# A four-layer graph network on one core: seven products for the first weight, and sums by adding DMA transfers for the third

## The chip, the core and the metric

The kernel runs on one core of a Trainium2 chip. The metric is device time in microseconds. One launch computes everything, from the inputs in the chip's memory to the output. TensorE (PE in the profile) multiplies matrices, with its weight loads shown as PEld; VectorE (DVE), ScalarE (ACT) and GpSimd (POOL) work elementwise; SyncE (SP) and GpSimd issue transfers (DMA). Each engine takes its own instructions in order, and waits for the others by semaphores.

## The reference

The input x is 128 graphs of 64 nodes with 256 features, fp32, and one 64 x 64 matrix `adj` is shared by all graphs. Four layers follow one another, each as `x = layernorm(x + layer(x))`. The change touches layer 0, and the computation of eigenvectors that is threaded into it and used in layer 1:

```python
def _slconv(x, adj, S, W):
    support = jnp.einsum('bnf,fh->bnh', x, W)
    weighting = adj * S                        # S is adj itself here
    return jnp.einsum('nm,bmh->bnh', weighting, support)

def layer0(x):
    h = relu(_slconv(x, adj, adj, W1))         # 256 -> 512
    h = relu(_slconv(h, adj, adj, W2))         # 512 -> 1024
    return _slconv(h, adj, adj, W3)            # 1024 -> 256

def layer1(x):
    deg = sum(A, 0) + sum(A, 1) - diagonal(A)
    L_norm = d_inv_sqrt[:, None] * (diag(deg) - A) * d_inv_sqrt[None, :]
    _, U = eigh(L_norm)                        # 64 x 64
    agg = einsum('mn,bnd->bmd', U.T, x)
    return einsum('nm,bmd->bnd', U, relu(agg @ W1 + b1) @ W2 + b2)
```

Layer 2 is a chain of graph convolutions and short LSTMs, layer 3 an attention among the nodes of a graph. Their instructions on PE, DVE and ACT stand in the same order before and after the change.

## The kernel before

**Groups.** Layer 0 works through 16 groups of 512 rows of x (8 graphs), in the order 4 to 15, then 0 to 3. A group goes through: `burst` (mixing by `adj`² over the nodes, which also transposes; 64 small matmuls in bursts) into `m1`; the first weight, `weigh`, into `h1` with a relu; `burst` into `m2`; the second weight into `h2`, with a relu; the third weight into `s3`; `mix_rows` (mixing again), the residual sum, and the layernorm in pieces (`scalar_norm`, seven pieces: five on ACT, one on POOL). The group g + 1 is interleaved with group g: its `burst` into `m1` stands in the middle of the second weight of g, its first weight among the products of the third weight of g, its `burst` into `m2` after that.

**Seven products.** The second weight (in two halves, `j` = 0 and 1) and the third are multiplied as 2 x 2 blocks by seven products in place of eight, with sums of blocks formed ahead by DVE: `sums_second` for the second weight, and for the third four sums of 1024 elements a partition out of `h2` (`sh[:, 0]`, `sh[:, 1]`, `H21` and `H12` in `layer0`). The sums of the weights are formed once (`sums_of_weights`). `seven` issues the products in the order 1, 2, 6, 5, 7, 3, 4. Products 1, 6, 7 and 4 add up in one PSUM bank (`ch`), 5 and 3 in another (`b5`), 2 has one of the four `ps` banks. Between them the partial results are taken out: ACT copies product 1 to block c11; DVE adds product 2 to it, and ACT applies the relu; ACT copies `ch` after product 6 to c12; ACT copies product 5 to c22; DVE adds `ch` after product 7 to c22; DVE adds product 3's to c12; and ACT takes `ch` after product 4 to c21. The first weight is not done so: per group it is eight matmuls of 512 columns. The last two groups' third weight (`PLAIN` = 2) is done by plain products, `plain`.

**Order.** In layer 0, the order of instructions on PE, DVE and ACT is the order in which the program gives them. `step` puts the eviction of a product behind the matmuls of the next one, and then appends one piece of the norm. Instructions of POOL and SP go to their own queues in the order in which they are given.

**Eigenvectors.** `eigen` computes U on the same engines: 62 steps of a tridiagonalisation (about 24 small DVE operations and one matmul pair each), six passes of bisection, recurrences, and a tail that ends with `u2` and `ut2`, which layer 1's first matmuls read. It is a Python generator. `mm` (L965) adds the stated time of each matmul to a clock `now`; `between` (L955) then lets `eigen` go on when the time that it last asked for has been reached. That time is what the DVE operations given so far sum up to by *stated* times: `Timed` (L42) adds `least` (0.25 us, 0.285 in the bisection, 0.22 in the recurrence) for each, plus a term for long ones. So stated times decide between which matmuls the operations stand, not how long they take.

In the profile L52 is any DVE operation of `eigen` or of layer 0, L966 any matmul given by `mm`, L1031 the matmuls of `burst`, L312 and L323 the matmuls of `eigen`, L162 any instruction of layers 1 to 3, L975 a relu, L1070, L1077 and L1081 the copies of `seven`, L1037 the copies of `burst`. Names in groups leave out buffer numbers: `m` is m1 or m2, `h` is h1 or h2, `aw` the weights, `tw` and `tv` sums of weights, `ss` and `sh` sums of blocks.

## Time and profile before

| | us |
|---|---|
| median of three timed runs (lowest to highest) | 2280.58 (2280.14 to 2281.84) |
| the profiled execution, its own time | 2277.23 |
| its span (first to last instruction) | 2275.4 |
| granted TensorE clock, mean | 0.995 |
| layer 0's matmuls in the span | about 25 to 828 |
| one group of layer 0 (from 309.90 to 360.37, the same products of two groups) | 50.47 |

The page cuts the span into 40 slices and gives each engine's busy share in tenths. Slices 1 to 14 are layer 0:

```profile
PE   8999999999999989999999999999999999999997
PEld 6888888887788778999999999999999999999985
DVE  5888777776888879765967977977877887578977
ACT  3444444443434435665655655655656555566554
POOL 0000000000000010000100000000010010000012
PEclk9999999999999999999999999999999999999999
DMA  7000000000000031000111211211221211001331
```

Two rows of its costliest groups show how layer 0's products are listed. The columns are line, engine, operation, output and inputs, shapes and count; then busy us in total and mean ns of one; then the idle time just before them with what ended most of it:

```profile
L966 PE MATMUL ch<-m,tw 128*128 128x256 f32 x512 | 124.7, 381 | 3.1 <-ACT h L1077 1.7
L966 PE MATMUL b<-ss,aw 128*128 128x256 f32 x512 | 121.9, 379 | 0.0
```

A matmul of fp32 leaves two records, so x512 are 256 matmuls.

### The profile page before, as it was taken

The numbers are of one execution on the slowest core, as the hardware profiler recorded it, in microseconds if no ns is written. First come the engines' busy times: TensorE is split into PE (matmuls) and PEld (weight loads), VectorE is DVE, ScalarE is ACT, GpSimd is POOL, SyncE is SP. The second block draws the span as 40 slices with busy tenths as digits, with TensorE's granted clock in tenths as the row PEclk, the third lists the DMA queues.
The fourth block names the chain that finished last, engine by engine and source line by source line (L and its number), as shares of the span: only waits on it lengthen the run. The fifth ranks groups of instructions, "written<-read, shape, count | busy, mean of one in ns | idle before, by whom it ended". The sixth has DMA issues, their size and how long they took to land.

```text
span 2275.4 us, 52244 instructions
## 1 busy us (share of the span) xinstructions
PE 2233.0 (98%) x20612; PEld 1990.8 (87%) x20612; DVE 1772.5 (78%) x5868; ACT 1189.5 (52%) x2892; POOL 137.0 (6%) x315
## 2 busy tenths in 40 slices
PE   8999999999999989999999999999999999999997
PEld 6888888887788778999999999999999999999985
DVE  5888777776888879765967977977877887578977
ACT  3444444443434435665655655655656555566554
POOL 0000000000000010000100000000010010000012
PEclk9999999999999999999999999999999999999999
DMA  7000000000000031000111211211221211001331
GB/s 245 11 11 11 11 11 11 11 20 11 11 11 1 1 126 57 11 11 20 66 40 48 78 57 50 87 57 41 87 66 40 78 66 39 31 21 65 117 107 59
DMA packets 80117, 107.93 MB, mean 47 GB/s; under 512 B 23296, under 2 KB 64256, under 8 KB 79872
## 3 DMA queue, kind: packets, MB, share of 16 engines
q1 hardware_dynamic: 79520, 104.32, 14.1%
q8 instruction: 162, 2.65, 0.5%
q14 instruction: 83, 0.68, 0.1%
q10 hardware_dynamic: 352, 0.28, 0.0%
HBM read 57.64 MB, written 45.09 MB: 45 GB/s over the span
## 4 chain that ended last, share of the span: by engine, by line
PE 91%; DVE 6%; issue 1%; ACT 1%; DMA 1%; POOL 0%; SPq 0%; ACTq 0%; DVEq 0%; POOLq 0%
PE ps L162 58%; PE ch L966 14%; PE ps L966 10%; PE b L966 7%; PE ps L1031 2%; PE pa L312 1%; DVE w L162 1%; DVE D L52 1%; DVE tw L52 1%; DVE X L162 1%; DVE gates L162 0%; DVE st L162 0%; DVE v L162 0%; ACT gates L162 0%; DVE h L52 0%
## 5 line engine op out<-in xcount | busy, mean ns | idle before, releaser
L162 PE MATMUL ps<-w,wih 128*128 128x128 f32 (+2 forms) x2944 | 572.0, 298 | 0.3 <-ACT gates L162 0.3
L162 PE MATMUL ps<-w,sums 128*128 128x128 f32 (+2 forms) x3104 | 476.3, 293 | 0.1
L162 PEld LDWEIGHTS ps<-w,wih 128*128 128x128 f32 x2944 | 453.1, 191 | 26.5 <-issue 6.8
L162 PEld LDWEIGHTS ps<-w,sums 128*128 128x128 f32 x3104 | 422.7, 191 | 14.3 <-ACT gates L162 1.9
L162 ACT ACTIVATE gates<-gates,cbi 128x256 f32<-128x256 f32 (+4 forms) x736 | 314.0, 479 | 171.8 <-DVE gates L162 169.9
L162 DVE TENSOR_TENSOR gates<-gates,ps 128x512 f32<-128x512 f32 (+4 forms) x408 | 233.7, 583 | 171.1 <-PE ps L162 158.0
L162 ACT COPY gates<-ps 128x512 f32<-128x512 f32 (+4 forms) x408 | 204.2, 506 | 252.3 <-PE ps L162 245.4
L162 PE MATMUL ps<-hs,whh 128*128 128x128 f32 (+1 forms) x896 | 181.2, 284 | 0.1
L162 PE MATMUL ps<-w,whh 128*128 128x128 f32 (+1 forms) x896 | 181.2, 284 | 0.0
L162 ACT ACTIVATE gates<-ps,cbi 128x128 f32<-128x128 f32 (+2 forms) x368 | 119.5, 384 | 42.9 <-PE ps L162 42.5
L162 PEld LDWEIGHTS ps<-hs,whh 128*128 128x128 f32 x896 | 139.8, 191 | 0.3 <-DVE hs L162 0.3
L162 PEld LDWEIGHTS ps<-w,whh 128*128 128x128 f32 x896 | 139.8, 191 | 0.0
L975 ACT ACTIVATE h<-h 128x512 f32<-128x512 f32 x96 | 60.5, 630 | 150.9 <-DVE h L52 150.9
L966 PE MATMUL ch<-m,tw 128*128 128x256 f32 x512 | 124.7, 381 | 3.1 <-ACT h L1077 1.7
L966 PE MATMUL b<-ss,aw 128*128 128x256 f32 x512 | 121.9, 379 | 0.0
L966 PE MATMUL ps<-aw,m 128*128 128x512 f32 x256 | 116.0, 606 | 1.5 <-DMA aw<-in_a_w_dram 1.5
L966 PEld LDWEIGHTS ch<-m,tw 128*128 128x128 f32 x512 | 94.9, 190 | 18.6 <-DVE h L52 3.4
L966 PEld LDWEIGHTS b<-ss,aw 128*128 128x128 f32 x512 | 96.8, 190 | 12.9
L162 POOL TENSOR_SCALAR rs<-mv 128x2 f32<-128x2 f32 x96 | 23.5, 255 | 1325.1 <-DVE mv L162 1323.7
L966 PEld LDWEIGHTS ps<-aw,m 128*128 128x128 f32 x256 | 48.3, 194 | 55.7 <-issue 51.4
L1037 ACT COPY m<-ps 128x512 f32<-128x512 f32 x96 | 51.2, 587 | 75.5 <-PE ps L1031 75.0
L162 PE MATMUL ps<-hs,sums 128*128 128x128 f32 (+1 forms) x448 | 90.6, 284 | 0.0
(373 smaller groups left out, 4139.2 us busy)
## 6 DMA issues: line engine op xcount, KB each, us to landing
far<-w SPq DMA_DIRECT2D x42, 512.0 KB, 2.9
w<-far SPq DMA_DIRECT2D x168, 128.0 KB, 3.1
X<-rest SPq DMA_DIRECT2D x24, 512.0 KB, 3.3
out_dram<-X SPq DMA_DIRECT2D x64, 128.0 KB, 1.8
rest<-XA SPq DMA_DIRECT2D x12, 512.0 KB, 2.6
rest<-X SPq DMA_DIRECT2D x12, 512.0 KB, 2.8
XA<-in_x_dram SPq DMA_DIRECT2D x22, 256.0 KB, 6.9
aw<-in_a_w_dram SPq DMA_DIRECT2D x3, 1024.0 KB, 10.2
```

The costliest lines, as they stand in the source:

```text
L52: return getattr(self.engine, name)(out, *args, **kw)
L162: getattr(e, name)(*[real(x) for x in args], **{k: real(v) for k, v in kw.items()})
L312: PE.matmul(out, lhsT, rhs, start=True, stop=True)
L966: PE.matmul(out, lhsT, rhs, start=start, stop=stop, **kw)
L975: S.activation(dst, src, AF.Relu)
L1031: PE.matmul(p[h][m, k, t, :], src[hs, t, f], sqT2[hs, hs], start=True, stop=True)
L1037: S.copy(to[:, h, c:c + 2], p[h])
```

## The change

- **First weight.** For the first weight of every group but the first in order, `seven` with `by_first` takes the place of `weigh`: products of 2 matmuls of 256 columns, 14 in all in place of 8 of 512. The blocks are quarters of `m1` (X11 to X22) and of W1. DVE forms sums of the blocks in `sums_first` (three operations of 256 elements) and one more (into X12) after product 2. Product 5 gets a `ps` bank. The seven products stand between products 2 and 5 of the third weight of the group before.
- **Third weight.** DVE's four sums are gone. ACT writes -H11 and -H12 (`less`, four operations a group) into two slots of `sh`; SP copies two blocks into the other slots (512 KB each); and five transfers of 512 KB a group, issued by GpSimd, add blocks in place (`adds`). `h2` is laid out again so that a block is contiguous in a partition. The order of its products becomes 1, 2, 5, 6, 7, 3, 4, and the two `burst`s into `m2` stand one place apart from before: after products 6 and 4. One group, not two, is done by `plain`.
- **Sums of weights.** Those of the second weight move ahead by two steps of the first weight, and those of the first weight are added after the first half of the second weight of the first group. The third's signs differ (`signed_sums`).
- **Eigenvectors.** The stated times go from 0.25 to 0.21, from 0.285 to 0.278, from 0.22 to 0.21 (layer 0's own operations stay at 0.25). In the tail, operations stand in another order, two squares become one operation, and the two last matrices are spread one at a time.

```diff
@@ -44,7 +44,7 @@
-        self.engine, self.free, self.until, self.least = engine, free, until, 0.25
+        self.engine, self.free, self.until, self.least = engine, free, until, 0.21
...
@@ -557,7 +557,7 @@
-    V.least = 0.285
+    V.least = 0.278
...
@@ -599,14 +599,14 @@
-    V.least = 0.22
+    V.least = 0.21
     for k in range(1, N):
-    V.least = 0.25
+    V.least = 0.21
...
@@ -704,29 +704,32 @@
+    V.tensor_copy(t1, pl)
+    pp_ = (yield from rows(co_[7], 1, "pa"))[:, 0, :]
+    there, until[0] = until[0], 0.0
     V.reciprocal(t0, t0)
     V.tensor_mul(t0, t0, C["off"])
-    V.tensor_copy(t1, pl)
     V.tensor_mul(t1, t1, t1)
     V.tensor_reduce(co_[8], t1, AX.X, ALU.max)
...
+    until[0] = max(until[0], there)
+    yield soon()
     rowdot(hs, pp_, t0)
     V.tensor_scalar(hs, hs, -1.0, 1.0, op0=ALU.mult, op1=ALU.add)
-    V.tensor_mul(hs, hs, hs)
-    V.tensor_mul(hs, hs, co_[8])
-    yield soon()
-    V.tensor_scalar(co_[9], s1, s1, 2.0, op0=ALU.mult, op1=ALU.mult)
...
     V.tensor_scalar(UT, pu, co_[12], None, op0=ALU.mult)
+    V.memset(u2, 0.0)
+    V.memset(ut2, 0.0)
     yield full()
+
+    def spread(out, lhsT):
+        p2 = ps([2 * N, N], "pa")
+        for h in range(2):
+            mm(p2[h * N:(h + 1) * N, :], lhsT, C["eye"])
+        for h in range(2):
+            V.tensor_copy(out[h * N:(h + 1) * N, h * N:(h + 1) * N], p2[h * N:(h + 1) * N, :])
+
+    spread(u2, UT)
     pt = ps([N, N], "pa")
     PE.transpose(pt, UT, C["eye"])
     until[0] = now[0] + 0.7
     U = cp.tile([N, N], F32, name="U")
     V.tensor_copy(U, pt)
-    V.memset(u2, 0.0)
-    V.memset(ut2, 0.0)
     yield full()
-    for out, lhsT in ((u2, UT), (ut2, U)):
-        p2 = ps([2 * N, N], "pa")
-        for h in range(2):
-            mm(p2[h * N:(h + 1) * N, :], lhsT, C["eye"])
-        for h in range(2):
-            V.tensor_copy(out[h * N:(h + 1) * N, h * N:(h + 1) * N], p2[h * N:(h + 1) * N, :])
+    spread(ut2, U)
 
 
 ROWS = 8192
...
-PLAIN = 2
@@ -983,24 +989,31 @@
     B11, B12, B21, B22 = (aw2[:, r:r + 2, c:c + 512] for r in (0, 2) for c in (0, 512))
     tw = wa.tile([P, 3, 2, 512], F32, name="tw")
     D11, D12, D21, D22 = (aw3[:, r:r + 4, c:c + P] for r in (0, 4) for c in (0, P))
-    tv = wa.tile([P, 4, 4, P], F32, name="tv")
+    tv = wa.tile([P, 5, 4, P], F32, name="tv")
+    W11, W12, W21, W22 = (aw1[:, r, c:c + 256] for r in (0, 1) for c in (0, 256))
+    tu = wa.tile([P, 3, 256], F32, name="tu")
     m1 = pa.tile([P, 2, 512], F32, name="m1")
     h1 = pa.tile([P, 4, 512], F32, name="h1")
     m2 = pa.tile([P, 4, 512], F32, name="m2")
     ss = pa.tile([P, 3, 2, 256], F32, name="ss")
-    h2 = pa.tile([P, 8, 512], F32, name="h2")
-    sh = pa.tile([P, 2, 4, 256], F32, name="sh")
+    h2 = pa.tile([P, 2, 8, 256], F32, name="h2")
+    sh = pa.tile([P, 4, 4, 256], F32, name="sh")
+    sx = pa.tile([P, 2, 256], F32, name="sx")
     s3 = pa.tile([P, 4, D], F32, name="s3")
     A11, A12, A21, A22 = (m2[:, k:k + 2, r:r + 256] for r in (0, 256) for k in (0, 2))
-    H11, H12, H21, H22 = (h2[:, c:c + 4, r:r + 256] for r in (0, 256) for c in (0, 4))
+    H11, H12, H21, H22 = (h2[:, r, c:c + 4, :] for r in (0, 1) for c in (0, 4))
 
 
     second = ((None, B11, B21, B22, tw[:, 2], B12, tw[:, 1], tw[:, 0]),
               (None, A11, A12, ss[:, 2], A22, ss[:, 0], ss[:, 1], A21))
-    third = ((None, D11, D21, D22, tv[:, 2], tv[:, 3], tv[:, 1], tv[:, 0]),
-             (None, H11, H12, H12, H22, sh[:, 0], sh[:, 1], H21))
+    third = ((None, D11, D21, tv[:, 4], tv[:, 2], tv[:, 3], tv[:, 1], tv[:, 0]),
+             (None, H11, H12, sh[:, 3], H22, sh[:, 0], sh[:, 1], sh[:, 2]))
+    X11, X12, X21, X22 = (m1[:, k, r:r + 256] for r in (0, 256) for k in (0, 1))
+    first = ((None, W11, W21, W22, tu[:, 2], W12, tu[:, 1], tu[:, 0]),
+             (None, X11, X12, X12, X22, sx[:, 0], sx[:, 1], X21))
     free = [0.0]
     VL = Timed(V, free, now)
+    VL.least = 0.25
     spare = [lambda: tl(pa, [P, D], "spare")]
     pending = []
 
@@ -1021,6 +1034,25 @@
         VL.tensor_sub(w[5], b12, w[1])
         VL.tensor_sub(w[6], w[3], w[5])
         VL.tensor_sub(w[4], w[2], w[6])
+
+    def signed_sums():
+        w = third[0]
+        VL.tensor_sub(w[7], D12, D22)
+        VL.tensor_sub(w[5], D12, D11)
+        VL.tensor_sub(w[6], D22, w[5])
+        VL.tensor_sub(w[4], D21, w[6])
+        VL.tensor_scalar(w[3], D22, -1.0, None, op0=ALU.mult)
+
+    def sums_first():
+        VL.tensor_add(sx[:, 0], X21, X22)
+        VL.tensor_sub(sx[:, 1], sx[:, 0], X11)
+        VL.tensor_sub(X21, X11, X21)
+
+    def less(slot, j, c):
+        S.activation(sh[:, slot, 2 * j:2 * j + 2], h2[:, 0, 4 * c + 2 * j:4 * c + 2 * j + 2, :], AF.Identity, scale=-1.0)
+
+    def adds(out, src):
+        nc.gpsimd.dma_start(out, src, accum_op=ALU.add)
 
     def burst(dst, src, c):
         to = dst.rearrange("p c (t h n) -> p h c t n", h=2, n=N)
@@ -1051,11 +1083,15 @@
 
         return product
 
+    def by_first(out, i, new):
+        w, a = (x[i] for x in first)
+        chained(out, [[(a[:, r * P:(r + 1) * P], w)] for r in range(2)], new)
+
     def by_third(out, i, new):
         w, a = (x[i] for x in third)
         chained(out, [[(a[:, k, r * P:(r + 1) * P], w[:, k, :]) for k in range(4)] for r in range(2)], new)
 
-    def seven(n, product, c11, c12, c21, c22, last):
+    def seven(n, product, c11, c12, c21, c22, last, order=(1, 2, 6, 5, 7, 3, 4), five="b5"):
 
         def view(b):
             return b[:, :2 * n].rearrange("p (i n) -> p i n", i=2)
@@ -1066,35 +1102,22 @@
                 relu(dst, dst)
 
         ch = view(bank("ch"))
-        product(ch, 1, True)
-        step(lambda: S.copy(c11, ch))
-        yield
-        b2 = view(bank())
-        product(b2, 2, True)
-        step(lambda: add(c11, b2))
-        yield
-        product(ch, 6, False)
-        step(lambda: S.copy(c12, ch))
-        yield
-        b5 = view(bank("b5"))
-        product(b5, 5, True)
-        step(lambda: S.copy(c22, b5))
-        yield
-        product(ch, 7, False)
-        step(lambda: add(c22, ch))
-        yield
-        product(b5, 3, False)
-        step(lambda: add(c12, b5))
-        yield
-        product(ch, 4, False)
-        step(lambda: last(c21, ch))
-        yield
+        for i in order:
+            if i in (2, 5):
+                b = view(bank("ps" if i == 2 else five))
+                b2, b5 = (b, None) if i == 2 else (b2, b)
+            out = {2: b2 if i == 2 else None, 5: b5 if i == 5 else None, 3: b5 if i == 3 else None}.get(i, ch)
+            product(out, i, i in (1, 2, 5))
+            step({1: lambda: S.copy(c11, ch), 2: lambda: add(c11, b2), 6: lambda: S.copy(c12, ch),
+                  5: lambda: S.copy(c22, b5), 7: lambda: add(c22, ch), 3: lambda: add(c12, b5),
+                  4: lambda: last(c21, ch)}[i])
+            yield i
 
     def plain():
         for t in (0, 2):
             p = bank().rearrange("p (t f) -> p t f", t=2)
             for i in range(2):
-                run(p[:, i, :], [(h2[:, c, (t + i) * P:(t + i + 1) * P], aw3[:, c, :]) for c in range(8)])
+                run(p[:, i, :], [(h2[:, t // 2, c, i * P:(i + 1) * P], aw3[:, c, :]) for c in range(8)])
                 step((lambda p=p, t=t: S.copy(s3[:, t:t + 2, :], p)) if i else None)
                 yield
         for _ in range(3):
@@ -1131,40 +1154,55 @@
         step()
         for t in range(4):
             weigh(t)
+            if t == 1:
+                sums_of_weights(second[0], B12)
         step()
-        sums_of_weights(second[0], B12)
         for c in (0, 2):
             burst(m2, h1, c)
         step()
         for g in range(n):
             sums_second()
             for j in range(2):
-                q = [h2[:, 4 * c + 2 * j:4 * c + 2 * j + 2, r:r + 256] for r in (0, 256) for c in (0, 1)]
-                for _ in seven(256, by_second(j), *q, relu):
-                    pass
+                q = [h2[:, r, 4 * c + 2 * j:4 * c + 2 * j + 2, :] for r in (0, 1) for c in (0, 1)]
+                for i in seven(256, by_second(j), *q, relu):
+                    if g == n - 1:
+                        continue
+                    if i == 5:
+                        less(2, j, 0)
+                    if i == 4:
+                        less(3, j, 1)
+                    if j and i == 7:
+                        nc.sync.dma_start(sh[:, 1], sh[:, 2])
+                    if j and i == 3:
+                        nc.sync.dma_start(sh[:, 0], H22)
+                        adds(sh[:, 1], H22)
+                    if j and i == 2:
+                        sums_first()
                 if j == 0 and g + 1 < n:
                     burst(m1, rows_of(order[g + 1]), 0)
                 if j == g == 0:
-                    sums_of_weights(third[0], D12)
-            q = [s3[:, r:r + 2, c:c + P] for r in (0, 2) for c in (0, P)]
-            w3 = seven(P, by_third, *q, S.copy) if g < n - PLAIN else plain()
-            next(w3)
-            next(w3)
-            if g < n - PLAIN:
-                VL.tensor_add(sh[:, 0], H21, H22)
-                VL.tensor_sub(sh[:, 1], sh[:, 0], H11)
-            for t in range(4):
-                if g + 1 < n:
-                    weigh(t)
-                if t == 0 and g < n - PLAIN:
-                    VL.tensor_sub(H21, H11, H21)
-                    VL.tensor_sub(H12, H12, sh[:, 1])
-            for _ in range(4):
+                    sums_of_weights(first[0], W12)
+                    signed_sums()
+            if g == n - 1:
+                for _ in plain():
+                    pass
+            else:
+                q = [s3[:, r:r + 2, c:c + P] for r in (0, 2) for c in (0, P)]
+                w3 = seven(P, by_third, *q, S.copy, order=(1, 2, 5, 6, 7, 3, 4))
                 next(w3)
-            if g + 1 < n:
+                for slot in range(3):
+                    adds(sh[:, slot], H21)
+                adds(sh[:, 3], sh[:, 1])
+                next(w3)
+                q = [h1[:, r:r + 2, c:c + 256] for r in (0, 2) for c in (0, 256)]
+                for i in seven(256, by_first, *q, relu, five="ps"):
+                    if i == 2:
+                        VL.tensor_sub(X12, X12, sx[:, 1])
+                next(w3)
+                next(w3)
                 burst(m2, h1, 0)
-            next(w3)
-            if g + 1 < n:
+                for _ in range(3):
+                    next(w3)
                 burst(m2, h1, 2)
             for t in (0, 2):
                 mix_rows(g, t)
-    nc = bacc.Bacc("TRN2", target_bir_lowering=False, num_devices=1, dynamic_dma_scratch_size=1024)
+    nc = bacc.Bacc("TRN2", target_bir_lowering=False, num_devices=1, dynamic_dma_scratch_size=1536)
```

More of the change, by code (lines that the diff above doesn't have):

```diff
@@ L712, in eigen @@
     V.tensor_scalar(co_[8], co_[8], nrm, (8.0 * 2.0 ** -24) ** 2, op0=ALU.mult, op1=ALU.mult)
-    pp_ = (yield from rows(co_[7], 1, "pa"))[:, 0, :]
+    yield soon()
+    V.tensor_scalar(co_[9], s1, s1, 2.0, op0=ALU.mult, op1=ALU.mult)
+    V.tensor_scalar(co_[10], s2e, s2e, 2.0, op0=ALU.mult, op1=ALU.mult)
+    V.tensor_tensor(co_[10], co_[10], co_[8], ALU.is_gt)
+    V.tensor_scalar(co_[11], s2e, 0.0, -2.0, op0=ALU.is_gt, op1=ALU.mult)
+    V.tensor_scalar(co_[11], co_[11], co_[10], 1.0, op0=ALU.mult, op1=ALU.add)
+    yield soon()
+    V.tensor_scalar(co_[12], s1, 0.0, -2.0, op0=ALU.is_gt, op1=ALU.mult)
+    V.tensor_scalar(co_[12], co_[12], 1.0, co_[11], op0=ALU.add, op1=ALU.subtract)
+    V.tensor_mul(co_[12], co_[12], rn)
+    V.tensor_mul(co_[11], co_[11], rn)
+    until[0] = max(until[0], there)
+    yield soon()
     rowdot(hs, pp_, t0)
     V.tensor_scalar(hs, hs, -1.0, 1.0, op0=ALU.mult, op1=ALU.add)
-    V.tensor_mul(hs, hs, hs)
-    V.tensor_mul(hs, hs, co_[8])
-    yield soon()
-    V.tensor_scalar(co_[9], s1, s1, 2.0, op0=ALU.mult, op1=ALU.mult)
+    V.tensor_scalar(hs, hs, hs, co_[8], op0=ALU.mult, op1=ALU.mult)
     V.tensor_tensor(co_[9], co_[9], hs, ALU.is_gt)
-    V.tensor_scalar(co_[10], s2e, s2e, 2.0, op0=ALU.mult, op1=ALU.mult)
-    V.tensor_tensor(co_[10], co_[10], co_[8], ALU.is_gt)
-    yield soon()
-    V.tensor_scalar(co_[11], s2e, 0.0, -2.0, op0=ALU.is_gt, op1=ALU.mult)
-    V.tensor_scalar(co_[11], co_[11], co_[10], 1.0, op0=ALU.mult, op1=ALU.add)
-    V.tensor_scalar(co_[12], s1, 0.0, -2.0, op0=ALU.is_gt, op1=ALU.mult)
-    V.tensor_scalar(co_[12], co_[12], 1.0, co_[11], op0=ALU.add, op1=ALU.subtract)
     V.tensor_scalar(co_[12], co_[12], co_[9], co_[11], op0=ALU.mult, op1=ALU.add)
-    V.tensor_mul(co_[12], co_[12], rn)
     yield full()
```

## The prediction

> **What bounds the kernel now.** I read the page's totals, then the windows of layer 0 (the only part whose instructions change: the order of the planned part, L162, is the same in both programs on PE, DVE and ACT), then the chain of waits, and last the timeline of one group and of layer 0's two ends.
>
> ```profile
> PE 2233.0 (98%) x20612; PEld 1990.8 (87%) x20612; DVE 1772.5 (78%) x5868; ACT 1189.5 (52%) x2892; POOL 137.0 (6%) x315
> PE 91%; DVE 6%; issue 1%; ACT 1%; DMA 1%; POOL 0%; SPq 0%; ACTq 0%; DVEq 0%; POOLq 0%
> ...
> core 0: us, PE busy (x) PEld busy (x) DVE busy (x) ACT busy (x) POOL busy (x), PEclk, DMA share, GB/s
> 57.00:541.00 484.00, 484.00 (x4319) 402.13 (x4319) 384.64 (x1794) 214.46 (x570) 20.33 (x56) 1.00 0.03 11
> 541.00:826.00 285.00, 282.35 (x2291) 230.65 (x2289) 237.89 (x874) 116.28 (x265) 14.21 (x37) 1.00 0.04 13
> 826.00:835.00 9.00, 4.59 (x48) 2.76 (x51) 7.17 (x35) 2.69 (x9) 1.08 (x3) 0.94 0.88 323
> ```
>
> From 57 to 541 TensorE has no gap at all, at a granted clock of 1.00; DVE is at 79% and ACT at 44%. Columns removed from TensorE are therefore time gained, one for one, as long as nothing takes a wait's place. At 826 to 835 TensorE is half idle: the eigenvectors come last. Prices of matmuls, from the chain of waits (start, us, what; the count is of records, two per matmul):
>
> ```profile
> 309.90 8.65 PE ps L966 x32
> 320.56 1.79 PE b L966 x16
> 334.17 1.73 PE ps L966 x8
> 812.36 13.81 PE ps L966 x64
> ```
>
> 1.73 is four matmuls of 256 columns (a product of the second weight). 1.79 is eight of 128 (one of the third). 8.65 is the third's product 2 and the four steps of the first weight together, so the first weight is 8.65 - 1.79 = 6.86 a group. 13.81 is a third weight without the seven products.
>
> **What the Trainium skill says.** "DMA: Bandwidth & Descriptors", section "Anatomy of one DMA — SWDGE (gpsimd) path", fits 2.0 us plus bytes/436e3 per transfer: 3.2 us for 512 KB. The trace agrees roughly, though on another queue: its 512 KB copies from SP take a median 2.9 us. The same page, "SWDGE vs HWDGE vs iDMA", says that adding transfers come from GpSimd only; that is how the change issues them. "Collectives: The Full Stack", "The bandwidth ceiling: the fold count and why AG ≠ RS ≠ AR", puts a reduction at half the rate of a copy, since each sum reads two sources. No run here shows it; it gives my estimate of an add's pace below. "SBUF — State Buffer", section "SBUF: two separate sides", warns that DVE can hold up the writing of GpSimd's descriptors. No trace here shows that either; it belongs to the second rival.
>
> **The change part by part.** Sums are against the profiled execution, 2277.23 us (span 2275.4); the median shown is 2280.58, so 3.35 is added at the end.
>
> First weight by seven, 15 groups (the first keeps the old way): a product is two matmuls of 256 columns, half of 1.73, and seven are 6.05. Gain 15 x (6.86 - 6.05) = 12.2. Group 14's third weight by seven: 13.81 - 7 x 1.79 = 1.3. TensorE loses 13.5 us of work.
>
> Its new waits. A product lasts 0.865 us now, half of the second weight's, but its evictions are as long as before. How the same order behaves there:
>
> ```profile
> 384.49 1.89 PE L966 MATMUL ps<-m,aw 128*128 128x256 f32 x8
> 387.06 0.67 DVE L52 TENSOR_TENSOR h<-h,ps 128x512 f32<-128x512 f32 x1
> 387.77 0.63 ACT L975 ACTIVATE h<-h 128x512 f32<-128x512 f32 x1 [2.00 <-DVE h L52]
> 388.31 0.49 ACT L810 ACTIVATE spare<-XA,sn_nm 128x256 f32<-128x256 f32 x1
> 388.93 0.57 ACT L1077 COPY h<-ch 128x512 f32<-128x512 f32 x1
> 391.39 1.89 PE L966 MATMUL b<-ss,aw 128*128 128x256 f32 x8
> ```
>
> Product 2 ends at 386.2. DVE's add follows at 387.06, ACT's relu 0.71 later, and what stands behind the relu on ACT 0.54 later still; ACT works in order. Behind it stands the copy of product 6 out of bank ch (0.57), and product 7 writes that bank. In the second weight product 7 begins 6.9 us in and never waits. In the first weight it is due at 3.47 (four products), while the copy ends at s + 0.71 + 0.54 + 0.6 and some 0.05 for the signal, s + 1.9, where s is the start of DVE's add, counted from the first product. DVE is late there: before the add stands the new subtraction into X12, which must wait until product 2 has read X12 (1.73, and 0.27 as DVE follows TensorE elsewhere: 2.00), then 0.30 for itself, then in 13 of the 15 groups two to five operations of the eigenvectors, 0.38 to 1.14 by their own rows. So s = 2.3 + (0 to 1.14), and TensorE stands for s - 1.55: 1.1 to 1.9 us with the eigenvectors beside it, 0.74 without. Over the 15 groups, by the operations that stand in the new program at each, 19.3. Product 4 then waits for the add of product 7, about 0.1 a group: 1.5. Together 20.8: more than the 13.5 removed. Nothing hides it, because TensorE takes its instructions in order and the third's products stand behind.
>
> Third weight's sums. DVE loses 14 x 4 operations of 1024 elements (1.14 us each in succession, 64 us), and gets 15 x (4 of 256 at 0.33 + 3 of 512 at 0.60) = 47. ACT gets four negations of 512 (0.59 each) and three relus more, about 4.2 a group against 22.8 busy of 50.5: hidden. The adds, counted from the end T0 of the second's last product: relu of H21 done at 1.2; four adds that follow land at 3.2 + k y (k = 1 to 4), 3.2 being that relu and 2.0 fixed. Needed by TensorE at 11.0, 12.8, 15.7 and 17.5 (the first's seven, with its stall, stands ahead). Cost of an add y: at least a copy's 1.2 (512 KB at the page's pace), twice that by its second source, 2.4, which I take: 12.8 against 17.5, hidden. The cover is gone at y = 3.6. The first of the five adds and the two copies go out before T0. SP's store of the group before stands between the copies, its data ready about 4 us ahead of T0; on POOL the roots of the norm go before the adds: neither delays.
>
> The eigenvectors. Their operations are placed by stated times. Alone an iteration takes DVE 5.0 us: 24 operations at 0.209 (319.26 to 324.28), stated 0.25 and now 0.21. It is slack today:
>
> ```profile
> 324.06 0.22 DVE L52 TENSOR_SCALAR u<-u,q 64x2 f32<-64x2 f32 x1
> 325.29 0.24 DVE L52 SCALAR_TENSOR_TENSOR junk<-pa,q,xr 64x29 f32<-64x29 f32 x1 [1.01 <-PE pa L312]
> ...
> DVE junk L52 <- PE pa L312: 41.6, 42, 4.0
> ```
>
> In the two programs' orders, at the paces above, 61 iterations hold 436.6 us of DVE work beside 509.9 of TensorE's (86%), afterwards 405.9 beside 421.7 (96%). Where DVE has more than TensorE locally the deficits add up to 1.8. I take 1.0 (from 0 to 10.6, fourth case). The eigenvectors' last matmuls move from TensorE's positions 783 to 800 us of 800 to 688 to 714 of 786. That frees layer 0's end:
>
> ```profile
> 826.36 1.98 PE L966 MATMUL ps<-s,sqT 128*128 128x512 f32 x4
> 832.39 0.28 DVE L52 TENSOR_SCALAR UT<-pa,co 64x64 f32<-64x64 f32 x1
> 834.18 0.38 PE L162 MATMUL ps<-u,X 64*64 64x64 f32 x2
> ```
>
> 5.8 us lie between the last mixing product's end and layer 1's first matmul; 1.4 of them are eigenvector matmuls that remain, so -4.4. What is late next is the norm of layer 0's last group, which may take back up to 2.
>
> The start. ACT's eviction of m stands behind a square root that waits for DVE's four sums of the second weight (18.6 to 23.5):
>
> ```profile
> 24.44 0.20 ACT L397 ACTIVATE q<-q 64x1 f32<-64x1 f32 x1 [4.26 <-DVE q L52]
> 25.64 0.79 PE L966 MATMUL ch<-m,aw 128*128 128x256 f32 x1 [3.57 <-ACT m L1037]
> ```
>
> Moved two steps of the first weight ahead, the sums begin earlier by some of this: -1.3 (from 0 to -2; the second weight's last half lands only at 16.3).
>
> Sum: -13.5 + 20.8 + 1.0 - 4.4 - 1.3 = +2.6; 2279.8 as profiled, 2283 as a median. About 0.2%, or 4.6 us, is what a measurement of this kernel can tell from no change.
>
> **The rivals.**
> Forecast, 0.55: the waits eat the gain; 2283, own range 2275 to 2291 (the stalls by 6 either way, the two ends by 3).
> Waits small, 0.18: if ACT passes on faster than in the second weight, or DVE reaches the add early, half of the 20.8 goes (2272) or all (2262); 2270 as its price. For it: DVE has slack of 41.6 us today. Against: the order of the two queues is fixed, and 0.71 + 0.54 is measured.
> Slow adds, 0.15, on the other side: the place is the third's product 3, which reads the last sum. With y = 4.0 it lands at 19.2 instead of 17.5: 1.7 x 15 = 26, so 2309. It decides from y = 3.6. For it: 75 adds with no row in this trace, and DVE, over 80% busy, may hold up their descriptors. Against: margin 4.7 us.
> DVE becomes the bound, 0.12: the 405.9 leave out each iteration's round over TensorE, some 0.43 (0.22 of matmuls, about 0.2 to be seen): 61 x 0.43 = 26, so 432 against 421.7, +10.6: 2294. Against: the stalls themselves give DVE time.
>
> **How the numbers follow.** The time is the forecast's. The range 2270 to 2306 leaves out the lower half of the second case and the upper half of the third, some 0.17. Faster: 0.12 of the forecast, 0.15 of the second: 0.27. Same: 0.25, 0.03 and 0.02: 0.30. Slower: 0.18, 0.15 and 0.10: 0.43.
>
> **What would show it.** In the new trace: in each group a gap on TensorE of 1 to 2 us ahead of the fifth product of 0.87 us, released by ACT; no gap ahead of the third's products 5, 6, 7 and 3 (a DMA as releaser there is the third case); layer 1's first matmul within 2 us of the last mixing product; the waits of DVE for pa far below 41.6. Gaps at pa on TensorE would be the fourth case. Wrong altogether: groups of 49.7 us without gaps.

## The result, and the profile after

The changed kernel takes 2322.65 us (median of four, 2319.16 to 2325.10) against 2280.61: ratio 1.0182, interval 1.0165 to 1.0200. Forecast were 2283, with a range to 2306, so the time lies outside. The loss is in layer 0: its last mixing product starts at 872.47, not 826.36, and layer 1's first matmul at 875.41, not 834.18. The rest of the program is 2.2 us longer.

First the totals and the chain of waits from the page of the changed kernel, then the windows over layer 0 (columns as before):

```profile
PE 2240.2 (97%) x20840; PEld 2022.1 (87%) x20840; DVE 1759.6 (76%) x5925; ACT 1238.9 (53%) x2999; POOL 205.6 (9%) x390
PE 79%; DVE 13%; ACT 3%; DMA 2%; issue 2%; SPq 1%; POOL 0%; DVEq 0%; ACTq 0%; POOLq 0%
```

```profile
57.00:541.00 484.00, 456.29 (x4120) 389.97 (x4118) 384.93 (x1948) 227.32 (x598) 60.37 (x96) 1.00 0.33 77
541.00:866.00 325.00, 316.54 (x2743) 273.63 (x2734) 230.15 (x812) 153.50 (x346) 41.79 (x71) 1.00 0.34 81
866.00:876.00 10.00, 9.24 (x76) 7.15 (x77) 1.58 (x3) 2.62 (x9) 0.00 (x0) 1.00 0.21 64
```

DVE's share of the chain rose from 6% to 13%, TensorE's fell from 91% to 79%. In the first window, where TensorE had no gap, it now stands for 27.7 us; DVE is busy for 385 us, as before: it is idle for a fifth of that window, and yet TensorE waits for it. What TensorE waits for over the whole run (us in total, times, longest), the first three lines:

```profile
PE ch L972 <- ACT h L1111: 22.1, 23, 5.0
PE ch L972 <- DVE h L52: 12.7, 17, 1.8
PE ch L972 <- DVE s L52: 4.3, 7, 1.3
```

TensorE's gaps up to layer 1 sum to 52.4 us, before to 17.2. That is 35.2 of the 41.2 by which layer 1 starts later. The other 6.0 are TensorE's own time, which was to fall by 13.5. The end of layer 0 did what was forecast:

```profile
872.47 1.96 PE L972 MATMUL ps<-s,sqT 128*128 128x512 f32 x4
...
875.41 0.81 PE L162 MATMUL ps<-u,X 64*64 64x64 f32 x39 [0.76 <-DVE rs_row L1226]
```

From the end of the last mixing product (874.27) to layer 1 it is 1.1 us now, where it was 5.8.

One group shows the new waits. Here is its timeline around the end of the second weight. Product 7 ends at 330.0, product 3 is the line at 330.02, product 4 the one at 332.90:

```profile
328.19 1.99 PE L972 MATMUL ch<-m,tw 128*128 128x256 f32 x8 [0.75 <-ACT h L1111]
329.29 0.15 DVE L52 RECIPROCAL q<-q 64x1 f32<-64x1 f32 x1 [1.16 <-ACT q L397]
...
330.02 1.46 PE L972 MATMUL b<-ss,aw 128*128 128x256 f32 x6
330.24 0.19 DVE L52 COPY LV<-u 64x64 f32<-64x64 f32 x1
...
331.36 0.22 DVE L52 TENSOR_SCALAR u<-u,q 64x2 f32<-64x2 f32 x1
331.74 0.23 DVE L52 SCALAR_TENSOR_TENSOR junk<-pa,q,xr 64x25 f32<-64x25 f32 x1 [0.16 <-PE pa L312]
332.02 0.23 DVE L52 SCALAR_TENSOR_TENSOR qr<-xr,q,pa 64x25 f32<-64x25 f32 x1
332.18 0.67 DVE L52 TENSOR_TENSOR h<-h,ch 128x512 f32<-128x512 f32 x1
332.90 1.99 PE L972 MATMUL ch<-m,tw 128*128 128x256 f32 x8 [0.77 <-DVE h L52]
```

DVE's add of product 7 could start when product 7 ends, at about 330.2. It stands behind a row of small eigenvector operations and starts at 332.18; product 4 may not write the bank before the add has read it. The eigenvector operations stand ahead of the add because `step` emits the add after product 3's matmuls: what `between` lets through beside product 3 gets into DVE's queue first.

The first weight's seven products of the same kernel, in a group without eigenvector matmuls (PEld is the weight load):

```profile
813.54 1.03 PE L972 MATMUL ch<-aw,m 128*128 128x256 f32 x4
814.40 1.03 PE L972 MATMUL ps<-aw,m 128*128 128x256 f32 x4
815.24 0.73 PEld L972 LDWEIGHTS ch<-tu,sx 128*128 128x128 f32 x4 [0.21 <-ACT h L1111]
815.27 1.10 PE L972 MATMUL ch<-tu,sx 128*128 128x256 f32 x4
816.21 1.03 PE L972 MATMUL ps<-aw,sx 128*128 128x256 f32 x4
817.68 0.73 PEld L972 LDWEIGHTS ch<-tu,m 128*128 128x128 f32 x4 [0.85 <-ACT h L1111]
817.68 1.13 PE L972 MATMUL ch<-tu,m 128*128 128x256 f32 x4 [0.44 <-ACT h L1111]
818.65 1.03 PE L972 MATMUL ps<-aw,m 128*128 128x256 f32 x4
819.66 1.13 PE L972 MATMUL ch<-tu,m 128*128 128x256 f32 x4
820.63 1.95 PE L972 MATMUL b<-tv,sh 128*128 128x128 f32 x16
```

The gap ahead of the fifth product, released by ACT, is the one forecast; the trace lists it as 0.44 to 1.83 us in the 15 groups. There is more. The first two products take 0.86 each (813.54 to 814.40). Those whose weight load had to wait, products 6, 7 and 4, take 0.94 to 0.97, and their load starts no more than 0.03 ahead of the matmul, elsewhere 0.1 to 0.2 ahead. (The 1.01 of product 3, from 818.65, holds the late start of product 4 behind it.) In all, the seven take 820.63 - 813.54 = 7.09. Nominal are 6.05, the listed gap is 0.44; the other 0.6 are such starts.

### The profile page after: what moved, and what is told of

Its sections match the earlier page's. It is cut to its first block, busy times and chain, and to the rows that moved or that the text cites. A ratio compares the mean times of both kernels' runs of the same rounds, so it can differ in the third digit from the quotient of the medians.

```text
span 2318.8 us, 53195 instructions
## 1 busy us (share of the span) xinstructions
PE 2240.2 (97%) x20840; PEld 2022.1 (87%) x20840; DVE 1759.6 (76%) x5925; ACT 1238.9 (53%) x2999; POOL 205.6 (9%) x390
## 4 chain that ended last, share of the span: by engine, by line
PE 79%; DVE 13%; ACT 3%; DMA 2%; issue 2%; SPq 1%; POOL 0%; DVEq 0%; ACTq 0%; POOLq 0%
PE ps L162 57%; PE ch L972 12%; PE ps L972 5%; PE b L972 4%; DVE h L52 2%; PE ps L1063 2%; DVE q L52 1%; DVE w L162 1%; DMA XA<-in_x_dram 1%; DVE xr L52 1%; DVE junk L52 1%; ACT h L981 1%; DMA sh<-sh 1%; DVE X L162 1%; DVE D L52 1%
## 5 line engine op out<-in xcount | busy, mean ns | idle before, releaser
L981 ACT ACTIVATE h<-h 128x512 f32<-128x512 f32 x141 | 88.9, 630 | 221.7 <-DVE h L52 221.6
L972 PE MATMUL ch<-m,tw 128*128 128x256 f32 x512 | 127.9, 389 | 21.8 <-DVE h L52 12.7
L972 PEld LDWEIGHTS b<-ss,aw 128*128 128x128 f32 x512 | 96.4, 190 | 12.7
L162 ACT ACTIVATE gates<-c 128x256 f32<-128x256 f32 (+1 forms) x176 | 75.5, 433 | 27.8 <-DVE c L162 26.5
L162 DVE TENSOR_TENSOR w<-w,w 128x128 f32<-128x128 f32 (+2 forms) x264 | 80.1, 313 | 7.8 <-PE ps L162 4.4
L162 DVE SCALAR_TENSOR_TENSOR c<-gates,c 128x256 f32<-128x256 f32 (+1 forms) x112 | 49.9, 445 | 41.0 <-ACT gates L162 40.8
```

Source lines behind the costliest of these rows:

```text
L162: getattr(e, name)(*[real(x) for x in args], **{k: real(v) for k, v in kw.items()})
L972: PE.matmul(out, lhsT, rhs, start=start, stop=stop, **kw)
L981: S.activation(dst, src, AF.Relu)
```

## The experiments

A group's period below is the distance of the same third product in two groups, read from TensorE's timeline; a gap is the idle time that the trace lists. Ratios are to the kernel before, with their 95% intervals.

| run | us | ratio (interval) |
|---|---|---|
| e1_old_times | 2303.08 | 1.0102 (1.0086 to 1.0119) |
| e2_no_first | 2332.97 | 1.0232 (1.0216 to 1.0247) |
| e3_times_only | 2299.35 | 1.0082 (1.0067 to 1.0097) |
| e4_third_only | 2298.33 | 1.0077 (1.0062 to 1.0092) |
| f1_war_fix | 2298.86 | 1.0087 (1.0072 to 1.0102) |
| f2_small | 2306.07 | 1.0114 (1.0098 to 1.0130) |
| f3_least23 | 2290.17 | 1.0046 (1.0031 to 1.0061) |
| f4_least27 | 2314.40 | 1.0151 (1.0135 to 1.0168) |
| g1_no_early | 2280.74 | 1.0007 (0.9998 to 1.0015) |
| g2_small_once | 2289.37 | 1.0042 (1.0027 to 1.0057) |
| g3_after_once | 2298.34 | 1.0083 (1.0067 to 1.0100) |
| g4_times_once | 2287.83 | 1.0034 (1.0022 to 1.0046) |
| h1_after_late | 2316.89 | 1.0167 (1.0152 to 1.0182) |
| h2_old_late | 2332.94 | 1.0238 (1.0221 to 1.0255) |
| h3_third_late | 2302.22 | 1.0106 (1.0091 to 1.0121) |
| h4_small_tail | 2278.44 | 0.9998 (0.9990 to 1.0007) |
| i1_small_held | 2282.45 | 1.0011 (1.0004 to 1.0018) |
| i2_tail_held | 2279.90 | 0.9999 (0.9990 to 1.0008) |

Where the time lies is read from TensorE's timelines of the profiled executions. "First group" is the start of product 2 of the first group's third weight, "groups" the time from there to the last mixing product, "end" the time from that to layer 1's first matmul:

| run | first group | groups | end |
|---|---|---|---|
| before | 57.4 | 769.0 | 7.8 |
| changed kernel | 62.1 | 810.4 | 2.9 |
| e1_old_times | 56.8 | 784.9 | 12.9 |
| e3_times_only | 58.5 | 792.2 | 2.9 |
| e4_third_only | 57.0 | 795.0 | 2.1 |
| f2_small | 60.2 | 787.6 | 10.5 |
| g1_no_early | 56.8 | 766.8 | 12.9 |
| g2_small_once | 60.0 | 771.8 | 12.0 |
| g3_after_once | 61.8 | 788.1 | 3.0 |
| h1_after_late | 55.7 | 814.6 | 3.0 |
| h2_old_late | 56.4 | 813.5 | 16.1 |
| h3_third_late | 57.6 | 798.7 | 2.1 |
| h4_small_tail | 55.7 | 767.8 | 9.0 |
| i1_small_held | 59.5 | 766.8 | 12.7 |
| i2_tail_held | 58.7 | 767.8 | 9.0 |

### Parts alone

**e1_old_times**: the changed kernel with the stated times of before.

```diff
-...least = engine, free, until, 0.21
+...least = engine, free, until, 0.25
-    V.least = 0.278
+    V.least = 0.285
-    V.least = 0.21
+    V.least = 0.22
...
-    V.least = 0.21
+    V.least = 0.25
```

> The changed kernel with the old stated times (0.25, 0.285, 0.22 us), all else changed. Theory 'packing' (the eigenvector operations, placed closer together, make DVE late, and TensorE waits for DVE in the second weight and in the third's last product): the 20 us of those waits go (12.2 and 3.7 in the second weight, 4.3 in the third), some of the 13.4 in the first's seven too, and the end of layer 0 gives back the 4.7 gained there: about 2305. Theory 'chain' (the first weight's seven products by themselves, with their additional work on ACT and DVE, cause the waits wherever they show): the waits stay, the end is lost: 2323 to 2328.

2303.08, as the theory "packing" had it. The new stated times cost 19.6 on top of the rest. That is a net figure: by the table they cost 5.3 in the first group and 25.5 in the groups, and the end gives 9.9 back. Groups take 51.3 to 52.5 us, against 52.9 to 58.8 of the changed kernel's groups with the tridiagonalisation.

**e2_no_first**: the first weight as before, its sums of blocks and of weights gone too, the rest of the change kept. (The lines of the edit that remove the sums are left out here.)

```diff
-                for i in seven(256, by_first, *q, relu, five="ps"):
-                    if i == 2:
-                        VL.tensor_sub(X12, X12, sx[:, 1])
+                for t in range(4):
+                    weigh(t)
```

> The changed kernel with the first weight as before, eight matmuls of 512 columns and no sums; third weight by transfers and new stated times stay. Theory 'chain': the waits of the first's seven (13.4) and those that follow from them (16 to 20) go, work on TensorE about 0.2 a group more: about 2290. Theory 'packing': the waits for DVE in the second weight stay to a good part, since the operations are as close as before: about 2305 to 2310.

2332.97, slower than the whole change and outside both expectations. Without the first weight's additional products, sums and evictions the waits for DVE grew (in the window 57 to 850 `ch` of the second weight 21.1 us, of the third 8.3). Neither theory as stated can explain that: less work made it later. The operations taken out had also advanced the stated clock, so that all later eigenvector operations stand elsewhere; e2 alone can't tell the two apart.

**e3_times_only**: the kernel before with `eigen` and its stated times as changed, nothing else.

> The kernel before with only the eigenvectors' part of the change (new stated times, new order at their end). Theory 'packing': DVE has 64 us more of work here than after the change, so the waits must show here too, by 10 to 30 us, and the end gains nothing or up to 4.7: 2285 to 2305. Theory 'chain': no new waits, and the eigenvectors end sooner: 2276 to 2279.

2299.35, as "packing" had it. Waits of the same two kinds, 11.3 us for DVE and 5.8 for ACT in the window 57 to 850, appear with none of the matmul changes.

**e4_third_only**: e1 and e2 together: third weight by transfers, small parts, old times, first weight as before.

> The third weight by transfers and ACT's negatives alone: first weight as before, old stated times. Both theories: no waits of the two kinds; DVE is relieved. TensorE's own time rises by 0.35 a group where products stand at waits (the sum of the third's products in the changed kernel is 13.06 us against 12.7), so 2281 to 2287. If the adding transfers cost more than that, it shows here alone: above 2290.

2298.33, above the 2287 of both theories and in the range kept for costly transfers. Waits for the transfers are 7.0 us in all (4.5 and 2.5 by the two lines of its waits); that the first weight ahead of the sums' readers takes 6.86 here and not 7.1 or more fits this, and is not shown to be the reason. But DVE and ACT are waited for by 8 us in the groups too, though DVE lost 64 us of sums.

### Density or place

A new pair of theories came from this: "density" (the operations stand too close) against "place" (what counts is where rows of them fall against the adds that TensorE needs).

**f1_war_fix**: e1 with the copy of product 6 ahead of the relu, in the first weight's seven alone.

```diff
+        def six():
+            S.copy(c12, ch)
+            while late:
+                late.pop(0)()
...
```

> The changed kernel with the old stated times, and in the first weight's seven ACT's copy of product 6 ahead of the relu of the first block, so that product 7 finds its bank free. Theory 'chain' (product 7 waits for what stands ahead of that copy on ACT): the gap ahead of product 7 (0.56 to 1.33 us in each group there, 11.6 in all) goes, and 0.1 a group for the start on a wait: 2303 becomes 2289 to 2292. If the gap only moves to product 4 (its bank is freed by DVE's add of product 7) less than half comes back: 2297 or more.

2298.86 (2297.60 to 2304.12), not separated from e1 by these runs (2301.72 to 2304.36), and short of what was expected. The gap did vanish: the line of ACT's copies is gone from the waits of TensorE in the groups. (The trace is of the slowest of the four executions, 2304.12.) Of its lines with e1 these matter here (window 57 to 850):

```profile
PE ch L972 <- ACT h L1111: 11.6, 15, 1.6
...
PE b L972 <- DMA sh<-sh: 1.2, 3, 0.5
```

and with f1 this is the first:

```profile
PE b L972 <- DMA sh<-sh: 7.2, 10, 1.5
```

The last adding transfer had been late behind the gap. With the gap gone it is what TensorE waits for: 6.0 of the 11.6 us came back there.

**f2_small**: the kernel before with the small parts: `eigen`'s tail, `PLAIN` = 1, and the sums of the second weight after the second step of the first weight.

```diff
         for t in range(4):
             weigh(t)
+            if t == 1:
+                sums_of_weights(second[0], B12)
         step()
-        sums_of_weights(second[0], B12)
```

> The kernel before with only the change's small parts: the sums of the second weight two steps earlier, the eigenvectors' new order at their end (old stated times), and one plain group in place of two. Both theories of the large parts: no effect of those here. -1 at the start, -1.3 for the group, 0 to -4 at the end: 2274 to 2279.

2306.07: 25 us slower, and a clear miss. Its groups have the same twelve records of eigenvector matmuls as before, so the density is the same; yet the first nine take 50.5 to 54.3, with gaps of 0.5 to 2.9 in seven of them. Of the 25 us, 20.8 lie in the groups and 3.5 in the first group (against g1 below).

**f3_least23** and **f4_least27**: the kernel before with 0.23 and 0.27 for `least`.

> The kernel before with the stated time of an eigenvector operation at 0.23 in place of 0.25 (bisection and recurrence as before). Theory 'density' (the closer the operations, the later DVE): about half of the 19 us that 0.21 cost: 2286 to 2292. Theory 'place' (what counts is where the bursts of operations fall against DVE's adds, and any other value spoils it): 2290 or more, as far as with 0.21.

> The kernel before with the stated time at 0.27. Theory 'density': no new waits in the groups, the eigenvectors end later, behind layer 0: 61 iterations of 24 operations later by 0.02 each are 29 us of stated time, of which what does not fit beside layer 0 shows at its end: 2281 to 2305, with groups of 50.5 us. Theory 'place': waits ahead of the last product of the second weight in the groups, groups above 51.

2290.17 and 2314.40. The first lies in the ranges of both theories and decides nothing; the second is above the range of "density". Looser operations have waits too: with 0.27, eight of the first ten groups have gaps (0.4 to 1.6), and TensorE stands at layer 0's end for the eigenvectors (15.8 and 12.4). Both neighbours of 0.25 are worse in the groups. 0.25 is not a limit of DVE; it is a value at which twelve records fall into each group at harmless places.

### The place, shown

**g1_no_early**: f2_small with the sums back at their old place.

> The kernel with the small parts (label f2_small) without the earlier sums of the second weight: only the eigenvectors' new order at their end and one plain group. Theory 'place' (what counts is where the eigenvector operations fall against DVE's adds; the earlier sums shift all of them): groups of 50.5 us without waits as in the kernel before, 2275 to 2281. Theory 'end' (the new order of the tail or group 14's seven products cost it): still above 2295.

2280.74; the first nine groups take 50.5 without a gap. The move of four operations alone made the 25 us.

**i1_small_held**: f2_small again, sums early, but their stated time entered at the old place, so that every later eigenvector operation stands where it stood in g1.

```diff
             if t == 1:
-                sums_of_weights(second[0], B12)
+                sums_of_weights(second[0], B12, V)
         step()
+        for _ in range(4):
+            free[0] = max(free[0], now[0]) + 0.25 + 0.0009 * 960
```

> The kernel f2_small (2306) with one difference: the four sums of the second weight still go out two steps of the first weight earlier, but their stated time is entered at the old place, so every later eigenvector operation stands where it stood in g1_no_early (2281). Theory 'place': 2277 to 2282, groups of 50.5 us. If the sums themselves, being earlier, cost (on DVE, or in the first group): 2295 or more.

2282.45, against 2306.07 for the same operations. The windows of 57 to 560, f2_small first:

```profile
57.00:560.00 503.00, 489.44 (x4322) 399.91 (x4321) 386.06 (x1800) 210.77 (x569) 19.38 (x54) 1.00 0.03 11
```

and i1_small_held:

```profile
57.00:560.00 503.00, 503.00 (x4475) 418.65 (x4473) 395.69 (x1860) 225.03 (x597) 21.95 (x60) 1.00 0.03 12
```

TensorE has no gap where DVE is busier (395.69), and 13.6 us of gaps where it is less busy. (The slower kernel gets through less in the window, so its DVE has less to do there; the work of a group is the same in both.) The hold is exact: up to 900 us the traces of i1 and g1 have the same order on TensorE and ACT, and on DVE from its 97th operation on, and the groups take 766.8 us in both.

The early sums themselves bring no gain. What they win at the start is lost at product 7 of the first group's second half. In g1, and then in i1:

```profile
47.16 0.35 DVE L1198 TENSOR_SCALAR wide_c_b<-wide_c_b,rs_col 128x256 f32<-128x256 f32 x1 [1.65 <-DMA wide_c_b<-in_c_b_dram]
49.30 1.99 PE L973 MATMUL ch<-m,tw 128*128 128x256 f32 x8 [0.23 <-ACT h L1084]
```

```profile
47.22 0.35 DVE L1201 TENSOR_SCALAR wide_c_b<-wide_c_b,rs_col 128x256 f32<-128x256 f32 x1 [1.65 <-DMA wide_c_b<-in_c_b_dram]
49.36 3.78 PE L973 MATMUL ch<-m,tw 128*128 128x256 f32 x8 [2.38 <-ACT h L1084]
```

In both, DVE stands for biases that a transfer brings, until 47.2, with the add of product 2 behind it; ACT's relu and the copy of product 6 follow that add, and product 7 starts at 49.3 however early TensorE came. Then i1's granted clock is 0.50 from 48.4 to 55.2; g1 has such a stretch from 23.3 to 30.1, ahead of this stop. The groups begin 2.7 us later in i1 than in g1, and 3.0 later in i2 than in h4 below. i1's interval against the kernel before, 1.0004 to 1.0018, is just above 1.

**g2_small_once**: f2_small, and DVE's adds of products 2 and 7 given ahead of the next product, so that eigenvector operations beside that product come behind them.

```diff
-        step(lambda: add(c11, b2))
+        step()
+        add(c11, b2)
...
-        step(lambda: add(c22, ch))
+        step()
+        add(c22, ch)
```

> The kernel with the small parts, and in every seven the two adds of DVE that follow products 2 and 7 put ahead of the next product in DVE's order, not behind it, so that eigenvector operations placed beside that next product no longer stand ahead of them. Theory 'place': the waits ahead of the last two products 'ch<-m,tw' (22 us in all) go in every group: 2275 to 2285. Theory 'density' (DVE has too much to do in these stretches, in whatever order): at most a third of it comes back, above 2295.

2289.37: 16.7 of the 25 are back, 15.8 of them in the groups; between the two expectations. Not the whole: gaps in the groups fall to 0 to 1.5, and what stays is at the start (3.9 once) and in starts on waits (the second to ninth group take 50.7 to 51.6 with hardly a listed gap). The edit is not one of order alone: an add's stated time is entered sooner with it, and by the traces 29 of 63 matmul pairs of the eigenvectors stand elsewhere than in f2, most by one or two matmuls (in g3, next, 26 of 63). What the adds' place is worth alone is therefore not shown as strictly as in i1.

**g3_after_once**: the same two adds, in the changed kernel.

> The changed kernel, all of it, with the same two adds put ahead. Theory 'place': the waits for DVE in the second weight (12.7) and most of those for ACT (22.1, of them 13.4 in the first's seven, where the relu no longer comes late) go: 2322 becomes 2290 to 2300. Theory 'density': DVE's load stays at 96% of TensorE's time, the waits only move to other products: above 2312.

2298.34, 24.3 less than the changed kernel. DVE's line in the waits of TensorE falls from 12.7 to 1.4 us; ACT's from 22.1 to 17.6, so less than I expected there.

**g4_times_once**: the kernel before with new times, small parts and the two adds.

> The kernel before with the new stated times, the small parts and the two adds put ahead. The new times alone made 2299. Theory 'place': 2270 to 2280, below the kernel before, since the eigenvectors end before layer 0 does. Theory 'density': DVE still late, 2290 or more.

2287.83. Between the two expectations. The groups have 0 to 2.0 us of gaps, now for ACT's copies. Against e3_times_only (2299.35) it is 11.5 better, with the small parts different too.

### What the two weights' changes do by themselves

**h1_after_late**, **h2_old_late**, **h3_third_late**: the changed kernel, e1 and e4 with the sums of the second weight back at their old place.

> The changed kernel with one line back at its old place: the sums of the second weight follow the whole first weight of the first group. On the kernel before, moving them cost 25 us with the other small parts (f2_small against g1_no_early), by shifting every eigenvector operation. Theory 'place, from the start': a good part of the change's loss is this one move: 2297 to 2308. Theory 'place, from each part' (the new stated times shift the operations anyway, and the move no longer matters): 2318 to 2326.

> The same with the old stated times too, so both weights' changes alone. Theory 'place, from the start': less than e1_old_times (2303), 2285 to 2295; what stays is the first seven's own: about 0.9 of waiting and 1 of starts on waits against 0.8 gained a group. Otherwise 2300 to 2306.

> The third weight by transfers alone, old stated times, sums of the second weight at their old place. With them moved it took 2298 (e4_third_only). If the transfers themselves cost (7 us of waits for them seen there, and starts on waits): 2290 to 2298. If the 18 us there were the move of the sums: 2278 to 2288.

2316.89, 2332.94 and 2302.22. The same move that costs 25 us on the kernel before gains 30 in e1 (2332.94 without it, 2303.08 with it). In e4 it gains 4 and in the changed kernel it costs 6, less clearly: the intervals of the ratios touch in the one case and overlap in the other. In the groups alone it costs 20.8 on the kernel before and gains 28.6 in e1, 3.7 in e4 and 4.2 in the changed kernel, whose 6 are lost in the first group (62.1 against 55.7). My expectations took its sign from one kernel; in the groups it has none. h2 and e1 differ in nothing but this move, and both hold twelve records in most groups. Their windows of 57 to 560, e1 and then h2:

```profile
57.00:560.00 503.00, 492.96 (x4527) 429.31 (x4525) 375.37 (x1851) 252.05 (x648) 65.06 (x106) 1.00 0.35 81
```

```profile
57.00:560.00 503.00, 472.30 (x4200) 404.64 (x4199) 359.09 (x1756) 233.78 (x616) 61.78 (x102) 1.00 0.34 80
```

Again there are more gaps where DVE is less busy, with the same work in a group.

So a cost of one part "by itself" can be read only where placement makes no gaps. In e1's groups at 676 and 726, past the last of the frequent eigenvector matmuls, the group takes 50.06 and 50.18; in the kernel before such a group takes 49.12. TensorE's nominal time is 0.81 less, the gap ahead of product 7 is 0.88, so 0.9 to 1.0 is left: starts on waits, in the first weight's products 6, 7, 3 and 4 (0.08 to 0.15 each) and the third's products from 6 on (0.09 to 0.10 each, 0.27 to 0.40 at product 7). Before, of the third's products only the last two, beside the `burst`s, show it, at 0.09 and 0.19.

**h4_small_tail** and **i2_tail_held**: g1 with 0.278 in the bisection and 0.21 in the recurrence, and the same with early sums and held clock.

> The kernel g1_no_early (small parts without the move) with the new stated times only where no group's placement hangs on them: bisection 0.278 and recurrence 0.21, tridiagonalisation at 0.25. Its groups keep their place; the eigenvectors' end comes 5 to 8 us sooner and TensorE's waits at layer 0's end (4.5, 2.2 and 0.9) go: 2272 to 2276, faster than both kernels. If the bisection's new place brings waits: 2279 to 2285.

> h4_small_tail (2278) with the same earlier sums and held clock. TensorE's wait of 3.6 us for ACT's copy at the start becomes about 2.1 as in the changed kernel: 2275 to 2278, at or a little below the kernel before.

2278.44 and 2279.90, both above what was expected: no difference from the kernel before that can be measured. In h4 the wait of 4.5 at layer 0's end is gone and layer 1 starts at 832.56, where g1's starts at 836.47; the time follows by 2.3, within the spread of both. No version here beats the kernel before.

## Why the prediction was wrong, point by point

- **The step that failed: "Where DVE has more than TensorE locally the deficits add up to 1.8. I take 1.0."** The sum compared amounts of DVE work with amounts of TensorE work between eigenvector iterations. The measured cost of the new times is 19.6 (the changed kernel against e1) and 19.2 (e3), after what they win at layer 0's end; in the groups alone 25.5 and 23.2. Amounts don't decide it: g1 and f2, i1 and f2, h2 and e1 have the same amounts and differ by 24 to 30 us. What decides is where the operations stand. In the gaps shown they stand ahead of DVE's adds in its queue, and with the adds put ahead (g3) 24 of the 42 us go.
- **"Moved two steps of the first weight ahead, the sums begin earlier ... -1.3 (from 0 to -2)."** TensorE's wait of 3.6 there becomes 2.1, but the gain does not reach the groups: they begin 4.7 later than before in the changed kernel, behind a wait of 5.0 at 53.4, and 2.7 and 3.0 later in i1 and i2, where only the sums moved. And I left out that these operations advance the stated clock that places every later eigenvector operation: +20.8 in the groups of the kernel before. In the groups of the changed kernel the same move gains 4.2, so it doesn't explain their loss.
- **First weight's seven, gain of 0.81 a group.** Right as nominal time. The term for waits was 19.3; measured are 13.4 in the window 57 to 826, by the mechanism forecast, which f1 confirms. With the tridiagonalisation beside it the gap is mostly 0.5 to 0.8 (1.62 and 1.83 twice) where 1.1 to 1.9 was forecast; in the four groups after it 0.87 to 0.98, and 1.26 once; in the last, at 813, which no eigenvector operation reaches, 0.44 where 0.74 was forecast.
- **"Product 4 then waits ... about 0.1 a group: 1.5".** This term was mis-sized: I gave such a cost to one product. Eight a group have a start on a wait in the two weights concerned, about 1.0 a group in clean groups, and the measured sum over layer 0 is larger: TensorE's own time rose by 6.0 instead of falling by 13.5.
- **Adding transfers.** Estimated 2.4 us each. The adds' queue took 9.0% of 16 engines' 2318.8 us for 75 of them: 2.78 each. But I let the four adds follow one another without a pause. The last, which reads the sum that another makes, is issued in 13 of the 15 groups only when all four ahead of it have landed, and then needs its own 4.7 us. In the group of 809.97 it is issued at 822.69 and TensorE waits until 827.80, which is 17.8 after the second's last product and not 12.8. In the changed kernel it was just hidden (1.1 us of waits); the case "slow adds" did not come about there, but f1 and e4 show how close it was (9.5 and 7.0 us of waits for transfers).
- **Layer 0's end.** -4.4 forecast, 5.8 to 1.1 measured: right.
- **The rival "DVE becomes the bound"**, 2294, named the right engine, and neither the place nor the reason. Its sign was gaps at `pa` on TensorE, and these are 0.8 us in all. Its reason was a total of 432 against 421.7, while DVE is idle for a fifth of the first window. (Its price counts the 1.0 of the forecast a second time: 2293.) The waits of DVE for `pa`, to fall far below 41.6, are 31.3.

What stays open: which of the 42 us belongs to which part. By the table 41.4 of them lie in the groups, 4.7 come from the first group, the end gives back 4.9, and the rest of the program adds some 2; but by parts of the change they don't add up (e3 and e4 lose 19 and 18, e2, which holds both, 53), and each shifts the placement of the others. Nor is it shown why 0.25 us happens to suit the kernel before.

## What to carry to other kernels

Where a second stream of small operations is threaded into an in-order queue by a stated clock, ask what stands ahead of each operation that the bottleneck waits for, and not only how much work the engine has: every edit that advances the clock, wherever it is, moves all that follows. Before judging such an edit, hold the placement (enter the old stated time at the old place, as i1 does), or make it matter less (give the awaited operation its place ahead of the next product, as g2 and g3 do: 17 and 24 us). When a start is to be made earlier, look for the next fixed stop behind it, here a transfer that DVE waits for. And price a product that starts on a wait, even a wait that is over by then, with about 0.1 us on TensorE: with short products this ate the gain.

## What the runs showed of the hardware

- A start on a wait costs TensorE about 0.1 us although no idle time is listed: products of 0.86 take 0.94 to 0.97, those of 1.79 take 1.88, where the weight load begins with the matmul and not 0.1 to 0.2 ahead of it.
- An adding transfer of 512 KB within SBUF, issued by GpSimd, takes the 16 DMA engines 2.78 us and lands a median of 4.7 (alone) to 6.7 (in a row) after its issue, against 2.9 for a plain copy of that size. "Collectives: The Full Stack", "The bandwidth ceiling: the fold count and why AG ≠ RS ≠ AR", in the Trainium skill, gives a reduction half a copy's rate. The runs agree: in the changed kernel a copy of 512 KB within SBUF, alone from 804.85 to 807.80, takes 44.0% of the engines' time there, 1.30 us, and an add, alone from 822.65 to 827.80, 54.2%, 2.79 us and 2.1 times as much.
- In the changed kernel DVE's operations keep their durations beside 75 such transfers (a 512-element add from `ps` 677 ns before, 678 after), so no hold-up of DVE by these transfers is seen. Whether DVE holds up the writing of their descriptors, which the prediction feared, was not tried.
- The granted clock of TensorE falls in single stretches of some us in the first group: 0.50 from 48.4 to 55.2 in i1, where four matmuls of 256 columns take 3.6 us from start to start of the next product (49.36 to 52.94), and 1.8 in g1 at a clock of 1.00 (49.30 to 51.13).
